# The inverse roots of a small position network: one GpSimd power in place of a Newton iteration on VectorE

## The chip, the cores and the metric

The kernel runs on one core of a Trainium2 chip. The metric is the device time of one execution in microseconds. Three runs of the kernel before gave 576.35, 576.94 and 577.33 us; the median is 576.94 us.

In the profile, PE is TensorE (matmul), PEld its weight loads, DVE is VectorE, ACT is ScalarE, POOL is GpSimd, and SP issues most of the transfers.

## What is computed

The input `x` has 4 sequences of 2048 rows with 256 columns. The reference does two things, each on a layer norm of `x` and each added back to `x`. The first is a gated Toeplitz operator:

```python
uv = silu(x @ uv_w); u, v = split(uv, 2)
out = u * _tno(v, rpe_params)          # a long convolution along the sequence, done by FFT there
return out @ o_w
```

The second is a product with eight groups of weights, `h2 = (x W1 + b1) W2 + b2`, with no nonlinearity between.

The coefficients of the convolution come from a small network that sees only the distance between two rows (4095 distances) and is the same for every sequence:

```python
def _ln(x, w, b):
    mu = mean(x, -1); var = mean((x - mu) ** 2, -1)
    return (x - mu) * rsqrt(var + 1e-5) * w + b

def _rpe(pos, ...):
    h = pos @ rpe_pos_w                       # 1 -> 32 features
    for i in range(3):
        h = silu(_ln(h, ln_w[i], ln_b[i])) @ fc_w[i]
    return silu(_ln(h, out_ln_w, out_ln_b)) @ out_w
```

So the network has four layer norms, and each needs `rsqrt(var + eps)` for every distance. That inverse root is what the change touches.

## The kernel before

**Layout of the network.** `rpe_network` (line 624) keeps its 4096 distances with the features on the partitions: four blocks of 32 features fill 128 partitions, and two tiles `k = 0, 1` of 512 columns hold the distances. The weights have been made free of their mean, so a layer's product needs no subtraction. A layer `i` runs like this:

- PE multiplies the block weights with `z` of the layer before: `ph`, 128x512, once per `k` (layer 0 multiplies the distances themselves).
- ACT squares `ph` (`sq`) and copies it (`d`). PE sums the squares with eight narrow matmuls into `pvar`: now the distances are on the partitions, 128 partitions by 32 columns. Layer 0 takes its variance from the squared distances `lag_p`, on DVE.
- `inverse_root` (line 608) turns the 128x32 variances into inverse roots. It works on DVE: an add of eps (`nve`); three operations that make a first guess out of the bits of the number (`nh`, `ny`, and `nve` times -0.5); then three rounds of Newton's iteration in `nt` and `ny`. The last product of the last round is left to the next step.
- That step (line 694) does the last product and spreads each root over the 32 features of its distance: `ne`, 128x512, once per `k`, on DVE.
- PE transposes `ne` back (`pr`, four transposes of 128x128 per `k`), DVE multiplies `d` by it, ACT applies `Silu` with the layer's scale and bias: `z`.

After the fourth layer PE transposes `z` (`pz`), DVE multiplies the decay in, and `rpe_transform` (line 724) brings the coefficients into the frequency domain: a chain of DVE sums (`eo`, `rcs` and others up to `rq`), matmuls `hp` with the matrices `mats_rpe`, products `tr` on DVE, matmuls `pa`. Nothing of the convolution can start without the result.

**What runs beside it.** The rest of the opening doesn't depend on the network:

- `stage_a` (line 573), once per quarter `q` of a sequence: statistics of `x`, the normalised `xn_a`, transposes `pt_a`, copies `xnt`, matmuls `pv` of `xnt` with `uvw`, `Silu` into `v`, sums and differences `c` on POOL. Its inverse root is already a power on POOL, of 128x4 numbers: `rs_a <- ve_a, mhalf`, where `mhalf` holds -0.5 (line 410).
- `stage_w` (line 843), once per weight group: multiplies the group's two matrices together into `pw` in eight steps, from loads `w` and after three small POOL operations `dw`.
- `gate` (line 905): matmuls `pu` and `Silu` into `gt`.

The convolution (`prepare` line 883, `stage_b` line 915) and the second half (`stage_d` line 1057) follow for each sequence.

At the start 20 matmuls on zeros (`warm`) keep PE running until the first data are there; each shows as two records.

**What sets the order.** No engine's queue is written by hand. Every call is recorded as an operation (line 76, which is why all rows of the profile bear the line 1155, where the recorded calls are issued). `issue_order` (line 287) then goes through all operations with a price for each and decides the order of every engine's queue; the ranks in `PLACE` (line 156) break ties. An engine works strictly along its queue, so an instruction that waits holds up all behind it. The price of a POOL operation is

```python
return (1000, 10) if ALU.pow in self.args else (140 + 2.15 * n, 40)
```

in nanoseconds, `n` being the columns: a power costs 1000 at any width. So the order in which the changed kernel's instructions stand is made for that price.

Of the kernel before, what the change touches and what calls it, by code (L numbers as in the profile page):

```python
# [31 lines left out]
F32 = mybir.dt.float32  # L32
I32 = mybir.dt.int32
AF = mybir.ActivationFunctionType
ALU = mybir.AluOpType
# [3 lines left out]
P = 128  # L39
# [3 lines left out]
F, L = 32, 3  # L43
# [3 lines left out]
NT = 32  # L47
# [322 lines left out]
def kernel(  # L370
# [21 lines left out]
    V, G, A, T, S = (Recorder(name, engine, ops) for name, engine in engines)  # L392

    def pool(name, bufs, **kw):
        return Pool(ctx.enter_context(tc.tile_pool(name=name, bufs=bufs, **kw)), name, bufs, tags)

    const = pool("const", bufs=1)
    io = pool("io", bufs=2)
    tok = pool("tok", bufs=2)
    small = pool("small", bufs=3)  # L400
# [8 lines left out]
    make_identity(nc, ident)  # L409
    mhalf = const.tile([P, 4], F32, name="mhalf")  # L410
    G.memset(mhalf, -0.5)
    eps = const.tile([P, 1], F32, name="eps")
    G.memset(eps, EPS)
    uvw = const.tile([P, 2, 2 * D], F32, name="uvw")
# [8 lines left out]
    def at(*key):  # L423
        ops.at(*place(*key))
# [3 lines left out]
    def t4(name, tag):  # L428
        return work.tile([P, 8 * P], F32, tag=tag, bufs=BUFS[tag], name=name)

    def t2(name, tag):
        return work.tile([P, 4 * P], F32, tag=tag, bufs=BUFS[tag], name=name)

    def load_x(b, q, tag):
        t = io.tile([P, 4, D], F32, tag=tag, name=f"{tag}_{b}_{q}")
        S.dma_start(t, x[b, q])
        return t
# [165 lines left out]

    NEWTON = 3

    def inverse_root(var, n, name):
        ve = small.tile([P, n], F32, tag="nve", bufs=2, name=f"nve_{name}")
        V.tensor_scalar_add(ve, var, EPS)  # L610
        y = small.tile([P, n], F32, tag="ny", bufs=2, name=f"ny_{name}")
        half = small.tile([P, n], F32, tag="nh", bufs=2, name=f"nh_{name}")
        V.tensor_single_scalar(half.bitcast(I32), ve.bitcast(I32), 1, ALU.logical_shift_right)
        V.tensor_scalar(y.bitcast(I32), half.bitcast(I32), -1.0, float(0x5F3759DF), ALU.mult, ALU.add)
        V.tensor_scalar_mul(ve, ve, -0.5)
        t = small.tile([P, n], F32, tag="nt", bufs=2, name=f"nt_{name}")
        for it in range(NEWTON):
            V.tensor_tensor(t, y, y, ALU.mult)
            V.tensor_tensor(t, t, ve, ALU.mult)
            if it < NEWTON - 1:  # L620
                V.scalar_tensor_tensor(y, t, 1.5, y, ALU.add, ALU.mult)
        return t, y

    def rpe_network():
        nw = 2 * (L + 1) + (L + 1) * F
        par = t4("par", "f4")[:, : nw + 8]
        S.dma_start(par, rpe_par)
        lnw, lnb = par[:, 0 : L + 1], par[:, L + 1 : 2 * L + 2]
        fcw = par[:, 2 * L + 2 : nw].rearrange("p (l f) -> p l f", f=F)
        lag_t = t4("lag_t", "i4")  # L630
        S.dma_start(lag_t[0:4, :], lag_rows)
        for q in range(2):
            at(f"a.{q}.x", 0)
            early[0, q] = load_x(0, q, "xa")
        at("rpe.d")
        decay = t4("decay", "f4")[:, :NT]
        S.dma_start(decay, decays)
        at("rpe")

        blk, seg = par[:, nw : nw + 4], par[:, nw + 4 :]  # L640
        mean = small.tile([P, L + 1], F32, tag="rmean", name="rmean")
        V.tensor_reduce(mean, fcw, AX.X, ALU.add)
        V.tensor_scalar_mul(mean, mean, 1.0 / F)
        V.tensor_tensor(fcw, fcw, mean[:, :, None].to_broadcast([P, L + 1, F]), ALU.subtract)
        w0 = t2("w0", "f2")[0:4, : 4 * F].rearrange("p (s f) -> p s f", f=F)
        V.tensor_tensor(
            w0, fcw[0:4, L : L + 1, :].to_broadcast([4, 4, F]), seg[0:4, :, None].to_broadcast([4, 4, F]), ALU.mult
        )
        bd = t2("bd", "f2")[:, : L * 4 * F].rearrange("p (l s f) -> p l s f", l=L, f=F)
        for i in range(L):  # L650
            V.tensor_tensor(
                bd[:, i], fcw[:, i : i + 1, :].to_broadcast([P, 4, F]), blk[:, :, None].to_broadcast([P, 4, F]), ALU.mult
            )
        V.tensor_scalar_mul(blk, blk, 1.0 / F)

        at("rpe.v")
        lag_p = small.tile([P, NT], F32, tag="lag_p", bufs=1, name="lag_p")
        S.dma_start(lag_p, lag_cols)
        V.tensor_tensor(lag_p, lag_p, lag_p, ALU.mult)
        wsq = small.tile([P, F], F32, tag="wsq", bufs=1, name="wsq")  # L660
        V.tensor_tensor(wsq, fcw[:, L, :], fcw[:, L, :], ALU.mult)
        wvar = small.tile([P, 1], F32, tag="wvar", bufs=1, name="wvar")
        V.tensor_reduce(wvar, wsq, AX.X, ALU.add)
        V.tensor_scalar_mul(wvar, wvar, 1.0 / F)
        V.tensor_scalar_mul(lag_p, lag_p, wvar)

        zs = [None, None]
        for i in range(L + 1):
            at(f"rpe.{i}")
            sqs, ds = [], []  # L670
            for k in range(2):
                ph = ps_f.tile([P, 4 * P], F32, tag="pf", name=f"ph{i}_{k}")
                if i == 0:
                    T.matmul(ph, w0.rearrange("p s f -> p (s f)"), lag_t[0:4, k * 4 * P : (k + 1) * 4 * P], start=True, stop=True)
                else:
                    T.matmul(ph, bd[:, i - 1].rearrange("p s f -> p (s f)"), zs[k], start=True, stop=True)
                if i:
                    sqs.append(t2(f"sq{i}_{k}", "e"))
                    A.activation(sqs[k], ph, AF.Square)
                ds.append(t2(f"d{i}_{k}", "rd"))  # L680
                A.copy(ds[k], ph)
            if i:
                pv = ps_i.tile([P, 8, 4], F32, tag="acc", name=f"pvar{i}")
                for c in range(8):
                    T.matmul(pv[:, c, :], sqs[c // 4][:, c % 4 * P : (c % 4 + 1) * P], blk, start=True, stop=True)
                var = pv.rearrange("p c s -> p (c s)")
            else:
                var = lag_p
            t, y = inverse_root(var, NT, f"{i}")
            for k in range(2):  # L690

                e = t2(f"ne{i}_{k}", "i2")
                t_, y_ = (a[:, k * 16 : (k + 1) * 16, None].to_broadcast([P, 16, F]) for a in (t, y))
                V.scalar_tensor_tensor(e.rearrange("p (n f) -> p n f", f=F), t_, 1.5, y_, ALU.add, ALU.mult)
                pr = ps_i.tile([P, 4 * P], F32, tag="acc", name=f"pr{i}_{k}")
                for c in range(4):
                    T.transpose(pr[:, c * P : (c + 1) * P], e[:, c * P : (c + 1) * P], ident)
                V.tensor_tensor(ds[k], ds[k], pr, ALU.mult)
                zs[k] = t2(f"z{i}_{k}", "e")
                A.activation(zs[k], ds[k], AF.Silu, bias=lnb[:, i : i + 1], scale=lnw[:, i : i + 1])  # L700

        at("rpe.z")
        z = t4("z", "i4").rearrange("p (j f) -> p j f", f=F)
        for k in range(2):
            pz = ps_i.tile([P, 4 * P], F32, tag="acc", name=f"pz_{k}")
            for c in range(4):
                T.transpose(pz[:, c * P : (c + 1) * P], zs[k][:, c * P : (c + 1) * P], ident)
            j = slice(k * 16, (k + 1) * 16)
            V.tensor_tensor(
                z[:, j], pz.rearrange("p (j f) -> p j f", f=F), decay[:, j, None].to_broadcast([P, 16, F]), ALU.mult  # L710
            )
        return z
# [403 lines left out]

    at("rpe")
    z = rpe_network()
    for q in range(NQ):
        stage_a(0, q)  # L1120
# [139 lines left out]
```

## Time and profile before

| what | value |
| --- | --- |
| median of three runs | 576.94 us |
| the profiled execution, time | 576.83 us |
| the profiled execution, span | 574.7 us |
| PE busy 15.0 to 56.2 us | 39.75 of 41.2 us |
| DVE busy 15.0 to 56.2 us | 23.82 of 41.2 us |
| POOL busy 15.0 to 56.2 us | 13.93 of 41.2 us |
| first `pr` of the four layers starts | 17.94, 28.48, 42.72, 53.17 us |
| `pz` starts | 56.19 us |

The stretch from 15.0 to 56.2 us reaches from the first matmul on real data of `stage_a` to `pz`, the end of the network proper. A row of the timeline gives start, duration, engine, line, operation, output and inputs, shape and how many instructions it joins; a row that joins several lasts from the first start to the last end. What stands in brackets is the idle time ahead of it and what ended that. The ends of matmuls are modelled, so starts say more than durations there.

### The profile page before, as it was taken

To read this page: it belongs to the slowest core of one execution; us is meant where nothing else is said; L and a number is where in the kernel's file an instruction comes from. 1 tells how busy PE (TensorE), PEld (TensorE's weight loads), DVE (VectorE), ACT (ScalarE), POOL (GpSimd) and SP (SyncE) were. 2 spreads that over 40 slices of the span, in tenths; PEclk is the share of its full clock that TensorE was granted. 3 is DMA by queue.
4 is the path that set the end of the run, shared out by engine and by line. 5 is a ranking of instruction groups with operands and counts; after the bars stand their busy time and mean duration, and the time that the engine had idled before them with its cause. 6 is when DMAs were issued, how large, how long until landed. Compare 5 with 4: busy or idle time off the path is not lost.

```text
span 574.7 us, 8343 instructions
## 1 busy us (share of the span) xinstructions
PE 562.7 (98%) x2676; PEld 460.4 (80%) x2676; DVE 506.3 (88%) x1122; ACT 310.9 (54%) x820; POOL 149.1 (26%) x184
## 2 busy tenths in 40 slices
PE   9999999999998999999999999999999999999997
PEld 6777667888887788888778788887887888878785
DVE  6485988999997999999977999999959999989963
ACT  3779683444242843958756617868658336211162
POOL 2054101010534220204563010206462021020410
PEclk9999999999999999999999999999999999999999
DMA  8642574544665235365251453545323553433212
GB/s 281 206 141 67 150 228 143 183 147 123 174 177 154 81 112 211 91 239 193 83 145 24 134 201 122 184 171 164 114 73 91 142 201 108 146 129 115 69 38 110
DMA packets 40195, 81.37 MB, mean 142 GB/s; under 512 B 5844, under 2 KB 7380, under 8 KB 40152
## 3 DMA queue, kind: packets, MB, share of 16 engines
q1 hardware_dynamic: 39416, 79.93, 44.6%
q10 hardware_dynamic: 736, 0.92, 0.5%
q8 instruction: 21, 0.34, 0.2%
q14 instruction: 22, 0.18, 0.1%
HBM read 72.44 MB, written 8.39 MB: 141 GB/s over the span
## 4 chain that ended last, share of the span: by engine, by line
PE 86%; DMA 5%; ACT 5%; issue 1%; DVE 1%; POOL 1%; SPq 0%; ACTq 0%; DVEq 0%
PE acc L1155 18%; PE pf L1155 17%; PE pff L1155 10%; PE po L1155 8%; PE pv L1155 8%; PE pu L1155 8%; PE pw L1155 7%; DMA w<-in_L_ffn_W_dram 4%; PE pt_d L1155 2%; PE pt_a L1155 2%; PE warm L1155 2%; PE pa L1155 1%; PE ph L1155 1%; DMA mats_rpe<-in_mats_dram 1%; PE hp L1155 1%
## 5 line engine op out<-in xcount | busy, mean ns | idle before, releaser
L1155 PE MATMUL acc<-mats,y 128*128 128x256 f32 (+1 forms) x512 | 114.5, 367 | 0.0
L1155 PEld LDWEIGHTS acc<-mats,y 128*128 128x128 f32 x512 | 91.8, 190 | 15.7 <-issue 3.9
L1155 POOL TENSOR_TENSOR gt<-gt,tk 128x512 f32<-128x512 f32 x32 | 44.9, 1413 | 114.0 <-DVE tk L1155 110.4
L1155 PE MATMUL pw<-w,w 128*128 128x256 f32 x256 | 62.5, 381 | 3.1 <-DMA w<-in_L_ffn_W_dram 2.2
L1155 PE MATMUL pv<-uvw,xnt 128*128 128x256 f32 x256 | 61.1, 380 | 1.1 <-ACT xnt L1155 1.1
L1155 PE MATMUL pu<-xnt,uvw 128*128 128x512 f32 x128 | 61.0, 594 | 0.0
L1155 POOL TENSOR_TENSOR c<-v 128x256 f32<-128x256 f32 x64 | 50.8, 821 | 39.3 <-ACT v L1155 25.2
L1155 PE MATMUL po<-ow,gt 128*128 128x256 f32 x256 | 60.7, 380 | 0.2 <-DVE xd L1155 0.2
L1155 PE MATMUL pff<-wt,xn 128*128 128x256 f32 x256 | 59.5, 382 | 0.7 <-ACT xn L1155 0.7
L1155 PE MATMUL pf<-ra,mats 128*128 128x256 f32 x256 | 59.5, 379 | 0.0
L1155 PEld LDWEIGHTS pw<-w,w 128*128 128x128 f32 x256 | 46.5, 190 | 12.5 <-ACT w L1155 4.2
L1155 ACT ACTIVATE w<-w,dw 128x256 f32<-128x256 f32 x64 | 29.5, 503 | 49.4 <-DMA w<-in_L_ffn_W_dram 46.3
L1155 PEld LDWEIGHTS pv<-uvw,xnt 128*128 128x128 f32 x256 | 47.9, 190 | 8.7 <-ACT xnt L1155 1.7
L1155 PEld LDWEIGHTS pff<-wt,xn 128*128 128x128 f32 x256 | 48.0, 190 | 8.4 <-ACT xn L1155 2.1
L1155 PEld LDWEIGHTS pf<-ra,mats 128*128 128x128 f32 x256 | 48.4, 190 | 7.1 <-PE po L1155 0.2
L1155 PEld LDWEIGHTS po<-ow,gt 128*128 128x128 f32 x256 | 47.4, 190 | 8.3 <-DVE xd L1155 1.1
L1155 DVE TENSOR_TENSOR y<-y,far 128x256 f32<-128x256 f32 x128 | 53.1, 453 | 0.1
L1155 POOL TENSOR_TENSOR rs_a<-ve_a,mhalf 128x4 f32<-128x4 f32 x16 | 20.0, 1247 | 122.1 <-ACT ve_a L1155 93.8
L1155 POOL TENSOR_TENSOR rs_d<-ve_d,mhalf 128x4 f32<-128x4 f32 x16 | 21.4, 1337 | 114.3 <-ACT ve_d L1155 97.2
L1155 ACT COPY e<-acc 128x512 f32<-128x512 f32 x24 | 14.0, 582 | 53.4 <-PE acc L1155 52.3
L1155 DVE TENSOR_TENSOR y<-pf,am 128x512 f32<-128x512 f32 x56 | 38.2, 682 | 3.5 <-PE pf L1155 3.4
L1155 ACT ACTIVATE gt<-pu 128x512 f32<-128x512 f32 x32 | 18.9, 592 | 39.3 <-PE pu L1155 37.0
(159 smaller groups left out, 1040.5 us busy)
## 6 DMA issues: line engine op xcount, KB each, us to landing
mats<-in_mats_dram SPq DMA_DIRECT2D x128, 256.0 KB, 2.8
w<-in_L_ffn_W_dram SPq DMA_DIRECT2D x64, 256.0 KB, 4.6
xa<-in_x_dram SPq DMA_DIRECT2D x18, 512.0 KB, 3.6
xd<-in_x_dram SPq DMA_DIRECT2D x14, 512.0 KB, 3.7
out_dram<-xd SPq DMA_DIRECT2D x12, 512.0 KB, 2.9
mats_rpe<-in_mats_dram SPq DMA_DIRECT2D x8, 256.0 KB, 4.6
row<-in_L_ffn_b_dram SPq DMA_DIRECT2D x8, 128.0 KB, 4.8
ph<-in_phases_dram SPq DMA_DIRECT2D x8, 128.0 KB, 5.3
```

Of the source, the lines that this page charges most:

```text
L1155: ops[k].call(*ops[k].args, **ops[k].kw)
```

## The change

`inverse_root` keeps the add of eps and does everything else with one power on POOL, 128x32 numbers to the power -0.5, from a second constant tile of that width. It returns the finished root, and the step after it copies the root over the features instead of doing the last product of the iteration. It is called four times, once per layer, with `n = 32`.

```diff
     mhalf = const.tile([P, 4], F32, name="mhalf")
     G.memset(mhalf, -0.5)
+    mhalf_n = const.tile([P, NT], F32, name="mhalfn")
+    G.memset(mhalf_n, -0.5)
...
     def inverse_root(var, n, name):
         ve = small.tile([P, n], F32, tag="nve", bufs=2, name=f"nve_{name}")
         V.tensor_scalar_add(ve, var, EPS)
         y = small.tile([P, n], F32, tag="ny", bufs=2, name=f"ny_{name}")
-        half = small.tile([P, n], F32, tag="nh", bufs=2, name=f"nh_{name}")
-        V.tensor_single_scalar(half.bitcast(I32), ve.bitcast(I32), 1, ALU.logical_shift_right)
-        V.tensor_scalar(y.bitcast(I32), half.bitcast(I32), -1.0, float(0x5F3759DF), ALU.mult, ALU.add)
-        V.tensor_scalar_mul(ve, ve, -0.5)
-        t = small.tile([P, n], F32, tag="nt", bufs=2, name=f"nt_{name}")
-        for it in range(NEWTON):
-            V.tensor_tensor(t, y, y, ALU.mult)
-            V.tensor_tensor(t, t, ve, ALU.mult)
-            if it < NEWTON - 1:
-                V.scalar_tensor_tensor(y, t, 1.5, y, ALU.add, ALU.mult)
-        return t, y
+        G.tensor_tensor(y, ve, mhalf_n, ALU.pow)
+        return y
...
-            t, y = inverse_root(var, NT, f"{i}")
+            y = inverse_root(var, NT, f"{i}")
             for k in range(2):
 
                 e = t2(f"ne{i}_{k}", "i2")
-                t_, y_ = (a[:, k * 16 : (k + 1) * 16, None].to_broadcast([P, 16, F]) for a in (t, y))
-                V.scalar_tensor_tensor(e.rearrange("p (n f) -> p n f", f=F), t_, 1.5, y_, ALU.add, ALU.mult)
+                V.tensor_copy(e.rearrange("p (n f) -> p n f", f=F), y[:, k * 16 : (k + 1) * 16, None].to_broadcast([P, 16, F]))
```

More of the change, by code (lines that the diff above doesn't have):

```diff
@@ L601, in stage_a @@
             G.tensor_tensor(c[:, 1 - r, j0 : j0 + 2, 1, :], a_, b_, ALU.subtract)
-    NEWTON = 3
     def inverse_root(var, n, name):
```

## The prediction

> **What bounds the kernel now.** I read the page first: its engine totals, its chain that ended last, its costliest groups. Then I took the timeline of the first 62 us, engine by engine, because the network runs only there, and last the views of single tiles.
>
> ```profile
> span 574.7 us, 8343 instructions
> ...
> PE 562.7 (98%) x2676; PEld 460.4 (80%) x2676; DVE 506.3 (88%) x1122; ACT 310.9 (54%) x820; POOL 149.1 (26%) x184
> ...
> PE 86%; DMA 5%; ACT 5%; issue 1%; DVE 1%; POOL 1%; SPq 0%; ACTq 0%; DVEq 0%
> ```
>
> TensorE (PE) is the bound: busy for 98% of the span and holding 86% of the chain. So what counts is not how much VectorE (DVE) work goes, but whether PE waits more or less. The network's second layer before the change looks like this on DVE and PE:
>
> ```profile
> 25.12 0.19 DVE L1155 TENSOR_SCALAR nve<-pvar 128x32 f32<-128x32 f32 x1 [5.18 <-PE pvar L1155]
> 25.34 0.18 DVE L1155 TENSOR_SCALAR nh<-nve 128x32 int32<-128x32 int32 x1
> ...
> 27.36 0.19 DVE L1155 TENSOR_TENSOR nt<-nt,nve 128x32 f32<-128x32 f32 x1
> 27.58 1.29 DVE L1155 SCALAR_TENSOR_TENSOR ne<-nt,ny 128x512 f32<-128x512 f32 x2
> 28.33 0.52 PEld L1155 LDWEIGHTS pr<-ident,ne 128*128 128x128 f32 x4
> 28.48 0.60 PE L1155 MATMUL pr<-ident,ne 128*128 128x128 f32 x4
> ```
>
> From `nve` to `ne` pass 27.58 - 25.12 = 2.46 us, and PE starts `pr` 0.90 us after `ne` starts. PE never stands still in it: transposes, `pw` and `pv` fill the time from 24.99 to 28.48. The fourth layer also takes 2.46 us (49.53 to 51.99); the third takes 5.48 us (35.63 to 41.11), because its small operations stretch to 0.45 to 0.77 us while POOL runs four `c` operations from 34.86 and four more from 38.85.
>
> **What the power costs.** No row shows a power on 32 columns. The rows for 4 columns:
>
> ```profile
> L1155 POOL TENSOR_TENSOR rs_a<-ve_a,mhalf x16: 1007/1022/2002, 10.2 to 404.8; 128x4 f32<-128x4 f32 x16
> L1155 POOL TENSOR_TENSOR nb_a<-nm_a,rs_a x12: 199/203/550, 58.6 to 406.5; 128x4 f32<-128x4 f32 x12
> ```
>
> The columns are minimum/median/maximum in ns. A power takes 1.007 us where a multiplication of the same shape takes 0.199. The 0.81 us between them is either a fixed price of a power, or 0.202 us for each of 4 columns. Lower bound: all fixed, about 1.0 us at 32 columns. Upper bound: all per column, 0.2 + 32 x 0.202 = 6.65 us. I take the upper end: POOL's plain rows are nearly proportional to their columns (`c`, 256 columns, some 0.70 us undisturbed; `gt`, 512 columns, 1.41 us), and a power is work on every element. In between lies a price such as 3.5 us.
>
> [...]
>
> **The change part by part.** Per layer, four times:
>
> Removed: eleven 128x32 DVE operations behind `nve` (three to seed, eight of the iteration), each 0.17 to 0.19 us undisturbed, 2.24 us from the first start to that of `ne` (25.34 to 27.58); the iteration's last product goes out of `ne` too. In the queues of the changed kernel as built, nothing else fills that room: DVE's next instruction is `ne`, which waits for POOL.
>
> Replaced: two `ne` (0.69 us each) by two copies 128x512 with a broadcast input. Rows: the copy from PSUM of that size takes 0.69 us; `rq` copies of 224 columns average 0.28 us and `rqd` of 64 columns 0.185, which extends to 0.45 at 512. Both inputs being in SBUF, I take 0.45. Only the first is ahead of `pr`: 0.24 us saved per layer, 1.0 us in all (0 at the other end).
>
> Added: a wait of DVE for POOL. Behind it stand the `d` products, and in layers three and four `nb_a_3`, then everything of the network. On POOL, behind the power, stand `dw` of the second weight group, `rs_a_1`, `rs_a_3` and the `c` operations; ACT's `w`, `xn_a` and `v` wait for those. Also added: a memset of 128x32, 0.1 us by the memset of 128x4, near 0.9 us; it is hidden, since POOL has nothing else from 1.34 until `ve_a` comes at 10.16.
>
> Moved: the planner prices a power at 1.0 us whatever its width, so it reorders the opening for a fast one. On PE two `pt_a_2` and half of `pv_1`, all of `pv_3` and `pu_0_0` go behind a later `pr`, `pvar` or `pz`. On SP the load of `b_3` passes `xa_1`, and `xa_0` and `b_5` go behind `w_3_0`; the SP queue otherwise stays. I price these moves at nothing: PE's own sum stays, and no PE wait of the opening but one of 0.99 us at 75.35 ends on a load. If that cover fails, the price is one load, 2.8 to 4.8 us.
>
> **The sum.** PE's work is priced by start-to-start spacing: a 128x256 matmul is two records of 0.216, so 0.43 (16 records from 49.71 to 53.17); four transposes 0.43; both `ph` 1.72; both `pvar` 1.73. I follow the changed PE queue with a power of 6.65 us, keeping the rows' delays from `pr` to `d` (0.72), `d` to `z` (about 0.85), `ph` to `sq` and `ne` to `pr` (0.90):
>
> - Layer 1: the second `rs_a` frees POOL at 13.38; power to 20.05; `pr` at 21.0. PE is done with three `pv` at 17.5: waits 3.5.
> - Layer 2: `ph` 23.6, `pvar` done 27.5, power 27.9 to 34.55, `pr` 35.5. PE has transposes and four `pw` until 30.5: waits 5.0.
> - Layer 3: `ph` 38.4, `pvar` done 42.7, power 43.1 to 49.75, `pr` 50.7. PE has two `pv` and four `pw` until 45.3: waits 5.4.
> - Layer 4: `ph` 53.6, `pvar` done 57.1; a `c` operation ahead of the power waits for `v_0`, so the power runs 57.9 to 64.55, `pr` 65.5. PE has work until 60.0: waits 5.5.
> - `pz` then comes at 68.8, against 56.2 before.
>
> Before, 38.1 us of PE work stood between 15.0 and 56.2: 3.1 us not used, by spacing. After, `pv_3` and `pu_0_0` (3.46 + 1.72) are still to do at 68.8. So PE is 68.8 - 56.2 + 5.2 = 17.8 us later for the same work. From `pz` on PE has 14.7 us of matmuls before `hp` and the DVE chain behind `z` takes some 12 (56.83 to 69.11), so PE stays the bound and nothing is made good, except that the wait of 0.99 us for `mats_rpe` (the only one from 56 to 120) goes, since that load no longer comes late: -1.0. Copies: -1.0.
>
> Last, the clock. The waits of 5 us have no like in the trace. The opening shows what a rested PE does:
>
> ```profile
> 1.19 6.96 PE L1155 MATMUL warm<-zeros 128*128 128x256 f32 x18 [1.19 <-DVE zeros L1155]
> ...
> 9.98 5.02 PE L1155 MATMUL warm<-zeros 128*128 128x256 f32 x22
> ```
>
> The same matmul comes every 0.387 us at first and every 0.221 (4.86 / 22, to the next at 14.84) later, while the granted clock stands at 1.00 in both: 18 x 0.166 = 3.0 us lost. After waits of up to 0.99 us no slow stretch follows. Bounds for three waits of 5 us: 0 and 3 x 3.0 = 9. I take one such loss, 3.0, since 5 us lie between the rows.
>
> [...]
>
> The profiled execution took 576.83 us, its span 574.7; the median of the three runs is 576.94, the same within 0.02%. Sum: 576.83 + 17.8 - 1.0 - 1.0 + 3.0 = **595.6 us**.
>
> **Rivals.**
> 1. *The power costs the same at 32 columns* (about 1.0 us). For it: all 16 `rs_a` have 4 columns, so a fixed part can't be excluded. In layer 1 the power follows `rs_a` at 13.4 and `ne` starts at 14.6, against 14.72: nothing won. PE stays busy by its queue; what can go is the 0.85 us before 42.18 and about half of the 0.99: 575.5 us, **faster**. This mechanism, POOL running the root beside DVE's queue, decides below about 1.7 us for a power, where the waits of 5 us above reach zero. That is the other side.
> 2. *A price between*, 3.5 us: each layer's wait shrinks by 3.15, to 0.35, 1.85, 2.25 and 2.35. That is 12.6 us less, and I count no slow clock for waits that short: 576.83 + 17.8 - 12.6 - 2.0 = 580.0.
> 3. *The power hides*, although slow, because PE has enough other work. It would need PE instructions moved ahead of each `pr`; the queue as built has 2.6 us of them in layers 2 and 3, against 8 us from `nve` to `pr`. I give this no more than a share of rival 1's chance.
>
> **How the numbers follow.** Per column: 0.64. A price between: 0.16. Fixed or hidden: 0.20, of which half ends below -0.2%. A measurement of this kernel can tell about 0.2% (1.15 us) from no change. So slower 0.80, same 0.09, faster 0.11. The likeliest case alone spans 591 (both small gains doubled, full clock) to 601.6 (two slow stretches more). The range reaches down to rival 1, 575.5, and up to 601, which leaves some 0.15 out.
>
> **What would show it.** Right: a POOL row `ny<-nve` near 6.6 us, four times; PE idle for 3 to 5.5 us before `pr`, released by DVE `ne`, itself by POOL `ny`; `pz` near 69; the same work after 120 us, shifted. Wrong: `ny` near 1 us, or POOL late because of `c` and not of the power. The clock step is right if matmuls after those waits come 0.43 apart instead of 0.216, wrong if none do.

## The result and the profile after

The changed kernel takes 593.18 us (median of four runs, 590.44 to 595.28) against 576.64 us for the kernel before beside it: a ratio of 1.0285, 95% interval 1.0237 to 1.0333. It is slower by 16.5 us; the prediction was 595.6. The profiled execution took 594.23 us. Below, medians and ranges are of all executions of a kernel, while ratios leave out the slow ones, over 1.5% above the kernel's fastest. The page of the profiled execution has these lines in place of those shown of before (engine totals, PE's busy tenths, the granted clock, the chain that ended last):

```profile
span 592.4 us, 8303 instructions
...
PE 567.9 (96%) x2676; PEld 464.4 (78%) x2676; DVE 498.3 (84%) x1078; ACT 311.9 (53%) x820; POOL 170.5 (29%) x189
...
PE   9778799999999999999999999999999999999997
...
PEclk9987899999999999999999999999999999999999
...
PE 86%; DMA 5%; POOL 4%; DVE 2%; ACT 2%; issue 1%; SPq 0%; ACTq 0%; DVEq 0%; POOLq 0%
```

The rows of PE and of its clock before:

```profile
PE   9999999999998999999999999999999999999997
...
PEclk9999999999999999999999999999999999999999
```

DVE has 8 us less to do, POOL 21 us more, and POOL now stands in the chain with 4%. Two things show in PE's rows that those of before don't have, both in the first 75 us (each digit is 14.8 us): PE is not always busy, and its granted clock, as a share of full speed, falls. The same 2676 matmul records also take 5.2 us longer.

The view of the roots `ny` (minimum/median/maximum in ns, then who waited for them) and PE's timeline of the opening show where:

```profile
L1145 DVE COPY ne<-ny x8: 419/426/946, 18.6 to 63.3; 128x512 f32<-128x512 f32 x8
L1145 POOL TENSOR_TENSOR ny<-nve,mhalfn x4: 5427/5429/5438, 13.2 to 56.9; 128x32 f32<-128x32 f32 x4
...
  DVE ne L1145: 21.2, 4
...
  PE pr L1145: 13.4, 4
```

```profile
19.12 0.66 PE L1145 MATMUL pr<-ident,ne 128*128 128x128 f32 x4 [2.35 <-DVE ne L1145]
...
32.03 1.69 PE L1145 MATMUL pr<-ident,ne 128*128 128x128 f32 x8 [3.33 <-DVE ne L1145]
33.51 3.02 PE L1145 MATMUL pv<-uvw,xnt 128*128 128x256 f32 x8
36.37 1.88 PE L1145 MATMUL ph<-z,bd 128*128 128x512 f32 x4
...
47.05 1.97 PE L1145 MATMUL pr<-ident,ne 128*128 128x128 f32 x8 [3.56 <-DVE ne L1145]
48.81 1.06 PE L1145 MATMUL pt_a<-ident,xn_a 128*128 128x128 f32 x4
49.66 2.77 PE L1145 MATMUL pw<-w,w 128*128 128x256 f32 x6
52.22 2.20 PE L1145 MATMUL ph<-z,bd 128*128 128x512 f32 x4
...
63.38 2.05 PE L1145 MATMUL pr<-ident,ne 128*128 128x128 f32 x8 [4.12 <-DVE ne L1145]
...
68.04 1.04 PE L1145 MATMUL pz<-ident,z 128*128 128x128 f32 x8
```

The power takes 5.43 us four times. DVE stands still for it for 21.2 us in all, and behind DVE's copies PE for 13.4 us; the first layer's wait was 2.35 us. The second thing is read from start to start: after the wait of 3.33 us, eight `pv` records take 36.37 - 33.51 = 2.86 us, 0.357 each, where before 16 such records took 3.46, 0.216 each. After the wait of 3.56 the six `pw` take 2.56 us, 0.43 each. That is half speed, and the granted clock over 15 to 69 us is 0.87.

The second layer, whose rows of before the prediction shows, now stands like this on POOL and DVE (DVE's timeline, then POOL's):

```profile
25.82 0.19 DVE L1145 TENSOR_SCALAR nve<-pvar 128x32 f32<-128x32 f32 x1 [4.37 <-PE pvar L1145]
...
31.55 0.76 DVE L1145 COPY ne<-ny 128x512 f32<-128x512 f32 x2 [5.54 <-POOL ny L1145]
```

```profile
26.09 5.43 POOL L1145 TENSOR_TENSOR ny<-nve,mhalfn 128x32 f32<-128x32 f32 x1 [6.62 <-DVE nve L1145]
```

From `nve` to `ne` pass 31.55 - 25.82 = 5.73 us, against 2.46 before. The eleven small operations were dearer in number than in time.

### The profile page after: what moved, and what is told of

Its sections match the earlier page's. It is cut to its first block, busy times and chain, and to the rows that moved or that the text cites. A ratio compares the mean times of both kernels' runs of the same rounds, so it can differ in the third digit from the quotient of the medians.

```text
span 592.4 us, 8303 instructions
## 1 busy us (share of the span) xinstructions
PE 567.9 (96%) x2676; PEld 464.4 (78%) x2676; DVE 498.3 (84%) x1078; ACT 311.9 (53%) x820; POOL 170.5 (29%) x189
## 4 chain that ended last, share of the span: by engine, by line
PE 86%; DMA 5%; POOL 4%; DVE 2%; ACT 2%; issue 1%; SPq 0%; ACTq 0%; DVEq 0%; POOLq 0%
PE pf L1145 18%; PE acc L1145 18%; PE pff L1145 10%; PE po L1145 9%; PE pu L1145 9%; PE pv L1145 8%; PE pw L1145 7%; DMA w<-in_L_ffn_W_dram 4%; POOL ny L1145 4%; PE pt_d L1145 2%; PE pt_a L1145 2%; PE pa L1145 1%; PE pr L1145 1%; DMA xa<-in_x_dram 1%; PE hp L1145 1%; PE ph L1145 1%
## 5 line engine op out<-in xcount | busy, mean ns | idle before, releaser
L1145 PE MATMUL pw<-w,w 128*128 128x256 f32 x256 | 63.9, 387 | 2.6 <-ACT w L1145 1.4
L1145 POOL TENSOR_TENSOR c<-v 128x256 f32<-128x256 f32 x64 | 52.0, 837 | 49.3 <-ACT v L1145 35.2
L1145 PE MATMUL pv<-uvw,xnt 128*128 128x256 f32 x256 | 62.8, 388 | 0.2 <-ACT xnt L1145 0.2
L1145 PEld LDWEIGHTS pv<-uvw,xnt 128*128 128x128 f32 x256 | 49.4, 196 | 8.0 <-issue 1.0
L1145 POOL TENSOR_TENSOR rs_d<-ve_d,mhalf 128x4 f32<-128x4 f32 x16 | 18.8, 1177 | 114.0 <-ACT ve_d L1145 96.9
L1145 ACT ACTIVATE xn_a<-xa,nb_a,rs_a 128x256 f32<-128x256 f32 x64 | 34.1, 596 | 10.4 <-POOL nb_a L1145 7.3
```

The costliest lines, as they stand in the source:

```text
L1145: ops[k].call(*ops[k].args, **ops[k].kw)
```

## The experiments

Theory A, the prediction's: the power has a price per column, PE waits for it, and a part of the loss is slow clock behind those waits. Its first rival, B: the loss comes from the new order of the queues, not from the power's length. Ratios are to the kernel before, run beside each. All except the three that change the planner's price and the two on the old iteration have the queues of the changed kernel, instruction for instruction, with the exceptions named.

**The length of the power, alone.** Three kernels differ only in the columns that the power works on: 4, 16 and 64 instead of 32.

```diff
-        G.tensor_tensor(y, ve, mhalf_n, ALU.pow)
+        G.tensor_tensor(y[:, 0:4], ve[:, 0:4], mhalf_n[:, 0:4], ALU.pow)
```

The copies then spread the roots that are there; with 16 columns the slices are `0:16`; with 64, two rows of exponents are raised over the 32 variances twice. Expected of 4 columns:

> The power works on 4 of the 32 columns only and the copies spread those 4 roots over all features, so 28 of 32 roots are left out; every queue holds the same instructions in the same order as in the changed kernel. Theory A (the power costs by the column, and PE's waits for it, with the slow clock after them, are the whole loss): ny takes 1.0 us, PE doesn't wait for ne more than 0.5 us, time 575.5 us (575 to 577), as rival 1 of the prediction reckoned. Rival B (the loss comes from handing the root from DVE to POOL and back, and from the order planned anew, whatever the width): 585 us or more.

Of 16 columns:

> The power works on 16 of the 32 columns, both copies read those 16 roots, so half of the roots is left out; queues as in the changed kernel. From 1.007 us at 4 and 5.43 at 32 columns the line is 0.375 + 0.158 per column: ny 2.9 us. Theory A with the slow clock: the four waits of 2.35, 3.33, 3.56 and 4.12 us shrink by 2.5 each, to 3.4 in all instead of 13.4, and no matmul runs at the slow rate any more, which was worth some 6 us: 593.2 - 10.0 - 6.2 = 577 us (576 to 579.5). Rival C (the slow clock costs nothing that isn't hidden in the waits): 593.2 - 10.0 = 583 us. Rival B: 593 us.

Of 64 columns:

> The suspected cost doubled: the power works on 64 columns (each root is taken twice, the second copy is not read); queues as in the changed kernel. Line of the power: 0.375 + 64 x 0.158 = 10.5 us. Theory A: four waits longer by 5.06 each, and a slow clock now after the first wait too (1 to 3 us): 593.2 + 20.2 + 2 = 615.5 us (613 to 618). Rival B: 593 us.

The power's rows, of these three kernels in turn:

```profile
L1145 POOL TENSOR_TENSOR ny<-nve,mhalfn x4: 1007/1010/1018, 12.9 to 43.3; 128x4 f32<-128x4 f32 x4
```

```profile
L1145 POOL TENSOR_TENSOR ny<-nve,mhalfn x4: 2901/2904/2909, 12.9 to 45.4; 128x16 f32<-128x16 f32 x4
```

```profile
L1145 POOL TENSOR_TENSOR ny<-nve,mhalfn x4: 10548/10551/10557, 12.8 to 74.0; 128x64 f32<-128x64 f32 x4
```

| columns | power, us | PE's waits for `ne`, us | clock | time, us (lowest to highest) | ratio (95%) |
| --- | --- | --- | --- | --- | --- |
| 4 | 1.01 | 0.2 | 0.999 | 574.19 (573.48 to 574.64) | 0.9963 (0.9951 to 0.9976) |
| 16 | 2.90 | 3.7 | 1.000 | 578.18 (577.0 to 581.61) | 1.0041 (1.002 to 1.0062) |
| 32, the change | 5.43 | 13.4 | 0.988 | 593.18 (590.44 to 595.28) | 1.0285 (1.0237 to 1.0333) |
| 64 | 10.55 | 33.9 | 0.969 | 615.3 (613.24 to 617.44) | 1.0676 (1.0645 to 1.0706) |

With the same order of all queues the time goes from a gain to a loss as the power gets longer, and the waits come out as they were expected. So the opening's new order isn't the cause, and B falls. Two steps differ in kind. From 4 to 16 columns the time grows by 4.0 us and PE's waits (of the profiled executions) by 3.5: the waits are nearly all. From 16 to 32 it grows by 15.0 and the waits by 9.7: 5.3 more than the waits explain, and there the clock falls. Missed by a little: 4 columns came out 1.3 us better than the 575.5 expected, and below its range.

**The slow clock, alone.** The changed kernel, with 7, 7 and 8 matmuls on zeros put ahead of the first `pr` of layers two to four, to take up PE's waits. They wait only for `nve`, so they run while the power does; `pr` still waits for the power. (The planner counts 1 ns for each of them, which keeps the order of all else.)

```diff
+    FILLERS = (0, 7, 7, 8)
...
+                if k == 0:
+                    for _ in range(FILLERS[i]):
+                        T.matmul(pr[:NT, : 2 * P], ve, zeros, start=True, stop=True)
```

> The changed kernel with idle matmuls in PE's waits: 7, 7 and 8 products of zeros (0.43 us each at the fast rate) ahead of the first pr of layers 2, 3 and 4, into the tile that pr overwrites; all else stands in the same order. They take up time that PE waits anyway, so they can only change the clock. Theory A with the slow clock: pr, pv, pw and ph behind the waits come 0.216 us per record again instead of 0.36 to 0.43, granted clock 1.00 from 28 to 69 us, the time falls by 4 to 6 us to 588 us (586.5 to 590), and the runs spread less than the 590.4 to 595.3 of the changed kernel. Rival C: 593 us or a little more, since PE has 9.5 us more work.

PE's second layer there with the later `pz`, and the span with the mean granted clock:

```profile
25.69 3.21 PE L1152 MATMUL pr<-zeros,nve 128*32 128x256 f32 x14
...
31.52 1.09 PE L1152 MATMUL pr<-ident,ne 128*128 128x128 f32 x8 [0.26 <-DVE ne L1152]
32.45 1.89 PE L1152 MATMUL pv<-uvw,xnt 128*128 128x256 f32 x8
34.18 1.88 PE L1152 MATMUL ph<-z,bd 128*128 128x512 f32 x4
...
62.15 1.04 PE L1152 MATMUL pz<-ident,z 128*128 128x128 f32 x8
```

```profile
core 0: 586.4 us, clock 1.000
```

It took 587.92 us (586.83 to 589.0), ratio 1.0203 (1.0186 to 1.022). The power takes 5.43 us as in the change and DVE waits 21.2 us for it as there, but the eight `pv` records after the wait come 0.216 us apart again (34.18 - 32.45 = 1.73). PE does more work and the kernel ends earlier: 593.18 - 587.92 = **5.3 us** of the loss are slow clock (4.7 us by the two ratios, each to the kernel before run beside). The profiled executions agree: from the `pr` of layer two to that of layer three, on to that of layer four and on to `pz`, the kernel with fillers is 1.69, 2.63 and 1.06 us shorter, 5.4 in all. This is no repair, since the waits, now filled with zeros, are still lost: 11.7 us more than the 576.22 of before beside it.

**An order made for the real price.** The planner is told what a power costs, so that it can put other PE work ahead of `pr`:

```diff
-        return (1000, 10) if ALU.pow in self.args else (140 + 2.15 * n, 40)
+        return (375 + 158 * n, 10) if ALU.pow in self.args else (140 + 2.15 * n, 40)
```

> The changed kernel with the planner's price of a power set to what was measured, 375 + 158 per column, instead of 1000 for any width; nothing else. The queues are then made for a slow root: pv_0, all of pt_a_2, pv_2 and more pw, pu stand ahead of the pr that they stood behind. Theory A (PE's in-order waits are the loss): most of it comes back, but the chain of a layer is still some 2.5 us longer than with the iteration (5.43 + 0.3 against 2.46, copies 0.24 less), so pz comes some 4 us later than the 56.2 of the kernel before, and DVE's chain of 12 us behind it decides: 577.5 to 581 us. Theory D (a root of 5.4 us can't be hidden behind other work in any order): 588 us or more.

Of its six executions three took 593.86 to 597.41 us and three some 603.3 (median 600.31); the ratio is 1.0347 (1.032 to 1.0374). That is no better than the change itself, and the sum by theory A falls. The waits for `ne` are gone, as the order meant it (0.2 us instead of 13.4), and others stand in their place. Of PE's waits in its profiled execution (total, times, longest):

```profile
PE po L1145 <- POOL gt L1145: 4.1, 2, 3.9
PE pw L1145 <- ACT w L1145: 2.9, 1, 2.9
PE ph L1145 <- ACT z L1145: 2.2, 1, 2.2
PE hp L1145 <- DVE rq L1145: 1.8, 1, 1.8
...
PE pr L1145 <- DVE ne L1145: 0.2, 1, 0.2
```

A second kernel adds to this the power in two halves of 16 columns, so that the first copy starts after 2.9 us:

```diff
-        G.tensor_tensor(y, ve, mhalf_n, ALU.pow)
+        for k in range(2):
+            c = slice(k * 16, (k + 1) * 16)
+            G.tensor_tensor(y[:, c], ve[:, c], mhalf_n[:, c], ALU.pow)
```

> As the kernel with the measured price, and the power in two of 16 columns each, so that the first half of a layer goes on 2.5 us earlier. Theory A: ny 2.9 us twice; the chain of a layer is shorter by up to 2 us than with one power; 575.5 to 578.5 us. Theory D: 588 us or more.

It took 593.0 us (592.06 to 595.81), ratio 1.0311 (1.0287 to 1.0335), far from the 577 expected. PE no longer waits for `ne` at all, but 4.2 us at `hp` for ACT's `junk_a`, 4.1 at `po` for `gt` and 3.0 at `pw` for `w`.

Is it the power or the order, then? The third kernel keeps the queues of the order made for the real price, every one instruction for instruction, and makes the power itself short: 4 columns.

> Every queue stands as in the kernel whose planner knows the measured price of a 32-column power (600.3 us, its profiled execution 595.6), but the power itself works on 4 of the 32 columns (28 of 32 roots are left out, the copies spread the four) and so takes 1.01 us instead of 5.43. What is open is where that kernel lost its time. E: partly to the order itself, late in the run and away from the power (TensorE stood still 3.4 us between 400 and 500 us, released by gt, and 1.6 us between 200 and 300, where the kernel after the change stood still 0.45 and 0.4), the rest, some 17 us, to layers that still last longer than the work between them: then the late waits remain and the early ones go, 574.2 + 4.2 = 578.5 us (577 to 582). F: to the power alone; the order is as good as the other one: 574 to 576. H: to the order alone, whatever the power takes: 588 or more.

Three executions took 593.96 to 595.5 us and three some 603 (median 599.1); the ratio is 1.036 (1.0314 to 1.0405). H holds and my own expectation, E, falls: the power went from 5.43 to 1.01 us and the time stayed. So this order costs about as much with the short power as with the long one, and no less than the change's waits did, and the price experiments say nothing of how well a long power could be hidden. Two of its waits lie far behind the network: 3.0 us at `pw` for ACT's `w`, ahead of which the chain has a load of the weights, and 3.9 us at `po` behind `gt`. In the kernel with 4 columns and the change's order no `pw` waits in 415 to 435 us and no `po` for `gt` in 550 to 566. In the profiled execution of the priced order PE stands still for 593.8 - 568.8 = 25.0 us, in that of 4 columns and priced order for 601.3 - 576.1 = 25.2, in that of 4 columns and the change's order for 572.4 - 561.4 = 11.0. The same 2676 records also keep PE busy longer than there, by 7.4 and 14.7 us, at granted clocks of 0.991 and 0.977 against 0.999. The order puts much other PE work ahead of the network: with 4 columns `pz` starts at 73.1 us in it, against 49.0 in the change's order. Which of its moves cost the time wasn't isolated.

The same wait shows something else. The two priced kernels, the wide power first, then the narrow one:

```profile
425.44 3.69 PE L1145 MATMUL pw<-w,w 128*128 128x256 f32 x16 [2.94 <-ACT w L1145]
```

```profile
429.49 6.65 PE L1147 MATMUL pw<-w,w 128*128 128x256 f32 x16 [3.02 <-ACT w L1147]
```

Sixteen equal records after nearly equal waits take 3.69 us in the one and 6.65 in the other, whose profiled execution is one of the longer ones (603.14 us, against 595.62). A wait of about 3 us is followed by a slow stretch in the second of these executions and not in the first (granted clock from 420 to 440 us 0.83 and 1.00); that fits the times of both kernels, of which each has some at 594 to 597 and some at 603 us. What the traces show beside the wait's length stands in the last section.

**The old iteration, two parts.** Could half of the change be kept? The kernel before with its last product at 128x32 and `ne` as the change's copy:

```diff
-            if it < NEWTON - 1:
-                V.scalar_tensor_tensor(y, t, 1.5, y, ALU.add, ALU.mult)
+            V.scalar_tensor_tensor(y, t, 1.5, y, ALU.add, ALU.mult)
...
-                V.scalar_tensor_tensor(e.rearrange("p (n f) -> p n f", f=F), t_, 1.5, y_, ALU.add, ALU.mult)
+                V.tensor_copy(e.rearrange("p (n f) -> p n f", f=F), y[:, k * 16 : (k + 1) * 16, None].to_broadcast([P, 16, F]))
```

> One part of the change alone: the iteration stays on DVE, its last product is done on 128x32 (0.19 us) and the two spreads are copies (0.42 instead of 0.69 us). The planner's order of the opening changes a little with it. The prediction's term says 0.24 us per layer less on the path for the copy; here 0.19 come back. Both theories: no difference that shows, 576.2 us (575.3 to 577).

It took 578.4 us (578.22 to 579.15), ratio 1.0051 (1.0036 to 1.0066), 2.2 us slower than expected. The copies take 0.43 us as they should, but the planner again makes another order, and in it `pz` starts at 58.6 us instead of 56.2. Which move costs this wasn't isolated.

The kernel before with two of Newton's rounds in place of three:

```diff
-    NEWTON = 3
+    NEWTON = 2
```

> The kernel before with two rounds of the iteration instead of three: a shorter root on DVE (3 of 11 operations less, 0.67 us per layer), no POOL. If the root's length on the path is what counts, this goes the way of the 1.0 us power, which took 574.2 us: 575.3 us (574.5 to 576.2). If the gain there came from DVE's operations that were gone, a quarter of it: 575.7 us. The two are too near to tell apart; the run asks whether a shorter root is worth anything with a whole computation.

It took 574.54 us (573.41 to 576.0), ratio 0.9982 (0.9971 to 0.9992): the only kernel with all its roots (each by one round less) that is ahead of both, if only by 0.2%. Its `pz` starts at 50.7 us, 5.5 us earlier than before, and some 1.4 us of that reach the end (575.91 beside it), as PE had been busy all the same. The planner made another order here too, so the shorter root and the order aren't told apart.

## Why the prediction was right, point by point

- **The bound and the path: right.** PE waits at `pr` behind DVE's `ne` behind POOL's `ny`, in all four layers. `pz` came at 68.04 us (68.8 predicted); `pr` at 19.12, 32.03, 47.05 and 63.38 (21.0, 35.5, 50.7, 65.5), 2 to 4 us early. That `pz` fits to 0.8 us is in part luck: the 68.8 held no slow clock, which the sum added afterwards, and the 68.04 holds it. In the kernel with fillers, where the clock stays full, `pz` starts at 62.15.
- **"I take the upper end", 6.65 us: mis-sized.** The power took 5.43. Four widths lie on one line, 0.375 us + 0.158 us per column (1.01, 2.90, 5.43, 10.55 us at 4, 16, 32, 64). The step read the fixed part from a multiplication, 0.2 us; a power has nearly twice that, so each of the 4 columns carried less. The waits came out at 2.35, 3.33, 3.56 and 4.12 us, 13.4 in place of 19.4; 4 x 1.22 = 4.9 of the 6.0 are the power.
- **"I take one such loss, 3.0": mis-sized the other way.** The kernel with fillers puts it at 5.3 us. The prediction took its size from the first `warm` records, with a granted clock of 1.00; but the first clock record of that profile lies at 6.90 us, and up to there the records come every 0.427 us, from there every 0.216. So that, too, was half speed. In the profiled execution all three waits over 3 us were followed by a slow stretch, with some 1.7, 2.9 and 1.6 us too much by start-to-start spacing. Without slow clock the loss is 11.7 us (587.92 - 576.22), where the sum had 17.8 - 2.0 = 15.8. So one part was 4.1 us too high, the other some 2 too low, and that the sum is off by only 2.4 us is to that extent luck.
- **The copies, -1.0: their size was right**, 0.426 us against 0.45. Only the two copies of layer four took longer, 0.94 and 0.95, beside POOL's `c` operations. What a shorter `ne` is worth at the end can't be told from noise here; with the old iteration it came with an order that lost 2 us.
- **"The wait of 0.99 us goes": not found.** That wait for `mats_rpe` is gone from PE's list, but others came, such as 1.4 us at `pa` for `tr`. From `pz` to the end pass 592.4 - 68.04 = 524.4 us, against 518.5 before plus 5.2 of moved work: 0.7 more, not 1.0 less.
- **The moves priced at nothing: right for this order.** With a power of 1.01 us and the same queues the kernel runs 0.4% faster than before. That is rival 1, measured: its 575.5 us were 574.2. It saw its mechanism decide below "about 1.7 us for a power". At 2.90 us the kernel is 0.4% slower, and a straight line between the two times, an estimate, meets that of before at about 2.0.
- **Rival 2's price, 3.5 us for 580.0:** 16 columns at 2.90 us took 578.2, and in its profiled execution, with waits up to 1.6 us, the clock stayed full.
- **Rival 3, that other PE work could hide the power:** the prediction gave it little, rightly for the queue as built. Whether some order could do it is open; the one that the planner makes for the true price loses as much elsewhere.

## What to carry to other kernels

In these runs fewer instructions on an engine off the critical path were worth only what they took out of the latency that the bound engine saw: eleven operations in 2.2 us were replaced by one in 5.4. Before an operation is used at another width, measure it at two widths; a row for one width hides how much of its price is fixed. And add to long waits of the matmul engine the slow matmuls behind them: here 5.3 us behind three waits of 3.33 to 4.12 us, 11.0 us together. Then mistrust a planner's new order as a free repair, since it is a change of its own.

## What the runs showed of the hardware

- A power on POOL took 1.01, 2.90, 5.43 and 10.55 us at 4, 16, 32 and 64 columns: some 0.158 us per column and a fixed 0.375. The four of the change hardly vary: 5427 to 5438 ns. The 4-column `rs_a` of the same profile vary more, from 1.006 to 2.003 us.
- The slow clock behind a wait isn't set by the wait's length alone. After 2.35 us in the first layer no slow records followed; after 3.33, 3.56 and 4.12 us they did; after 3.02 us they did in one kernel's profiled execution, after 2.94 us in another's they didn't. In the priced order a wait of 2.20 us, with three of 0.24 to 0.68 us shortly before it, was followed by four `ph` records in 3.13 us, against 1.88 in that kernel's next layer.
- What goes with it shows when the trace is cut where the granted clock changes. In the changed kernel these moments lie at 32.38, 35.79, 46.03, 52.86, 63.10 and 66.51 us, 3.41, 10.24, 6.83, 10.24 and 3.41 us apart, whole multiples of 3.41, and at 592.16, the kernel's end. In the trace of before the clock changes once, at 573.51 us. Four such stretches of the changed kernel and what came behind the last three (PE's busy time and records, granted clock, then the DMA):

```profile
core 0: us, PE busy (x), PEclk, DMA share, GB/s
15.31:18.72 3.41, 1.46 (x6) 1.00 1.03 314
28.96:32.38 3.42, 0.35 (x3) 1.00 0.43 136
32.38:35.79 3.41, 3.41 (x13) 0.50 0.33 97
42.62:46.03 3.41, 0.87 (x5) 1.00 0.27 76
46.03:52.86 6.83, 5.81 (x19) 0.50 0.66 157
59.68:63.10 3.42, 0.00 (x0) 1.00 0.43 144
63.10:66.51 3.41, 3.12 (x12) 0.50 0.00 0
```

- The stretch with the wait of 2.35 us had PE busy for 43% of it, and the clock stayed full; behind those with 10, 26 and 0% it was half. In the trace of before, half clock followed a stretch of 3.42 us with PE busy for 23% (570.09 to 573.51 us), at the kernel's end.
- Half clock was also seen without such a wait. In the run with the iteration's last product at 128x32, PE is busy for 24.65 of the 25.0 us from 15 to 40 us, yet the granted clock over them is 0.93, and four `pw` records take 1.70 us from start to start (26.87 to 28.57), 0.43 each. In the profiled execution of the order made for the real price, PE is busy for 29.51 of the 30 us from 40 to 70 us, with one wait of 1.00 us at 40.18; the clock is 0.94, and eight `pt_a` records take 1.94 us from start to start (44.34 to 46.28), against 0.87 for the eight at 51.02. Both follow the narrow `pvar` matmuls (4 columns) of a layer; whether such matmuls count for less isn't tested.
- The time spreads less where the clock stays full: 4.8 us over the changed kernel's four runs, 2.2 us with the fillers. The clock isn't all of that spread, since three of those four runs have 0.988 and lie between 590.44 and 594.23 us.
